# Square-root iteration of 1024 matrices with a convolution behind it: in images 19 to 31 the first quartic's square is turned by VectorE and DMA instead of TensorE

## The chip, the core and the metric

The kernel runs on one core of one Trainium2 chip, as one program. The metric is the time of one execution on the device in microseconds (us). A core has five engines with queues of their own: TensorE (PE; its weight loads are listed apart as PEld), VectorE (DVE), ScalarE (ACT), GpSimd (POOL) and SyncE (SP), and 16 DMA engines that move data between the chip's large memory (DRAM here) and its working memory SBUF, or inside SBUF. TensorE writes to PSUM, which has eight banks of 128 x 512 numbers.

## What is computed

x has 32 images of 32 channels of 128 x 128 numbers. Two layers are computed; only the first matters for this change. Cut down:

```python
def _L0_conv_ref(A):                      # A: 1024 matrices of 128 x 128
    normA = sqrt(sum(A2 * A2)); Y = A2 / normA; Z = I
    for _ in range(5):
        T = 0.5 * (3.0 * I - Z @ Y)
        Y = Y @ T
        Z = T @ Z
    return Y * sqrt(normA)

x = x + _L0_conv_ref(_gn(x))              # _gn: group norm, 16 groups of 2 channels
x = x + _L1_conv_ref(_gn(x), weights1, weights2)   # FFT, products by weights, inverse FFT
```

All numbers are 32-bit floats. Each matrix product of the first layer is four instructions of one bank: four channels form a group, and an image has eight groups.

## The kernel before, in words

The five iterations are rewritten as polynomials (`newton`, line 462). A group first gets a quartic polynomial q of its normalized matrix m, then y = m q, then the next m from y and q, then a second quartic of that, and at the end two short products that give the square root, which is added to the input tile xt. Since m isn't symmetric, a product needs one factor in transposed form; mb is the transposed companion of m.

There are two ways to make a quartic. `near_quartic` (line 407) is used for image 0 and images 19 to 31: v = square of m less a multiple of m, out of PSUM by DVE; r = mb + eye on POOL; v transposed by TensorE (`transposed(v)`: four instructions against the identity); w = that plus r, by DVE; then the product v w plus eye gives q. `far_quartic` (line 442) is used for images 1 to 18 in both quartics: the bare square is turned out of PSUM by one DVE instruction that transposes 32 x 32 blocks (`turned`, line 421), written to DRAM (`away`), and read back in another order (`back`) so that the blocks change places; v is made apart, by a DVE multiply-add onto a tile that POOL prepared as eye_v - mb, and POOL makes eye_q - m. No TensorE transposition is needed there, but two DMAs of 256 KB per quartic.

The order of the work is written out by hand. Each group is a Python generator, a lane, and each `yield` ends its share of a round. The main loop (line 1115) goes round the lanes; every engine runs its instructions in the order in which the loop issues them. A near lane is started every 5 rounds, a far lane every 3 (`NEAR`, `FAR`, line 42), and at most five near ones are under way. `yield from rest` is two rounds. Between lanes the loop steps the staging of later groups (`staged`, line 375, which scales xt into m and the second input tile into mb), the statistics of later images (`prep`, which loads xs on ACT's queue), the work behind a finished group (`settle`: a store to mid, folds on POOL; `forward`, `spectrum`), the products with weights, and `inverse` (line 953), which loads 512 KB tiles yt and results ob, adds and stores out. When a lane is started, `stage` also calls `fetch` (line 366) for a later group: two loads of 256 KB, which stand on SP's queue for far images and on ACT's for the others. `FIRST` is 19, the first image of the late stage.

Tiles come from `four` (line 312): `rooms` gives for each name how many buffers lie in the pool that stays (first number) and how many in a pool that exists until 158 groups have settled (second number); after that only the first number is left. A tile waits until the last reader of the buffer it takes is done.

Of the kernel before, what the change touches and what calls it, by code (L numbers as in the profile page):

```python
# [36 lines left out]
P = 128  # L37
# [56 lines left out]
def conv_preact_kernel(  # L94
# [84 lines left out]
    def bank():  # L179
        return ps8.tile([P, 4, P], F32, tag="ps", name="ps")  # L180
# [38 lines left out]
    def kept(issued):  # L219
        return issued  # L220
# [84 lines left out]
        yield  # L305


    rooms = dict(b=(4, 6), xt=(10, 5), x=(3, 2), r=(4, 0), v=(3, 2), w=(3, 2), q=(4, 2))
    rooms.update(my=(4, 3), mb=(2, 4), t=(3, 2), y4=(2, 2), turn=(0, 4))
    turns = dict.fromkeys(rooms, 0)  # L310

    def four(tag, more):
        n, m = rooms[tag]
        shape = [P, 4, 2, P] if tag == "my" else [P, 4, P]
        if more:
            turns[tag] += 1
            if turns[tag] % (n + m) >= n:
                return early.tile(shape, F32, tag=tag + "_early", name=tag, bufs=m)
        return sets.tile(shape, F32, tag=tag, name=tag, bufs=n)
# [20 lines left out]
    def minus(eye, m, t):  # L340

        nc.gpsimd.tensor_tensor(t, eye, m, ALU.subtract)
        return t
# [13 lines left out]
    def is_far(b):  # L357
        return 0 < b < FIRST

    def has_more(b, g):  # L360

        return b * (C // 4) + g < MORE
# [1 line left out]
    raw = {}  # L364

    def fetch(b, g):
        queue = nc.sync if is_far(b) else nc.scalar
        xt, t = four("xt", has_more(b, g)), four("b", has_more(b, g))
        kept(queue.dma_start(out=t, in_=x[b, :, 4 * g : 4 * g + 4, :]))
        kept(queue.dma_start(out=xt, in_=xt_in[b, :, 4 * g : 4 * g + 4, :]))  # L370
        raw[b, g] = xt, t
# [3 lines left out]
    def staged(b, g, nm, sc, off, sn):  # L375

        m = four("x", has_more(b, g))
        xt, mb = raw.pop((b, g))

        def on_scalar(t, x, offset, scale, c):  # L380
            c = slice(c, c + 1)
            kept(
                nc.scalar.activation(t, x, AF.Identity, bias=offset[:, c], scale=scale[:, c])
            )

        for j in range(4):
            c = 4 * g + j
            if j < 2 or not is_far(b):
                kept(
                    nc.gpsimd.tensor_scalar(  # L390
                        m[:, j, :],
                        xt[:, j, :],
                        nm[:, c // 2 : c // 2 + 1],
                        sc[:, c : c + 1],
                        ALU.add,
                        ALU.mult,
                    )
                )
            else:
                on_scalar(m[:, j, :], xt[:, j, :], off, sc, c)  # L400
            on_scalar(mb[:, j, :], mb[:, j, :], off, sc, c)
            yield
        v = minus(eye_v, mb, four("v", True)) if is_far(b) else None
        ready.append((xt, m, mb, v))
        yield

# [14 lines left out]
    def turned(ps, more):  # L421

        t = four("turn", more)
        nc.vector.transpose(blocks(t), ps.rearrange("p c (i b) -> p b c i", b=4))
        return t
# [13 lines left out]
    def by_rows(t):  # L439
        return blocks(t).rearrange("p a c j -> p c a j")  # L440

    def far_quartic(m, mb, v, f, later, more):

        ps = products(m, mb)
        held = away(turned(ps, more))
        if later:
            yield
        nc.vector.scalar_tensor_tensor(v, ps, 1 / (9 * MS), v, ALU.mult, ALU.add)
        if not later:
            yield  # L450
        minus(eye_q, m, m)
        yield
        w = back(held, "w", more)
        yield
        yield from rest
        q = plus(products(v, by_rows(w)), 9 / (39 * MS**2 * f**2), m, "q", more)
        yield from rest
        return q

    rest = (None, None)  # L460

    def newton(g, sn, xt, m, mb, v, far, more):


        qf, et, eye_t = (QS, EYE_Q, eye_q) if far else (QF, EYE, eye)
        if far:
            q = yield from far_quartic(m, mb, v, 1.0, False, more)
        else:
            q = yield from near_quartic(m, mb, more)
        my = four("my", more)  # L470
        y = my[:, :, 0, :]
        nc.scalar.mul(y, products(q, mb if far else m), 1 / (MS * qf))
        yield from rest
        m = my[:, :, 1, :]
        ps = products(y, q) if far else products(q, y)
        if far:
            held = away(turned(ps, more))
            yield
            nc.scalar.mul(m, ps, MS / qf)
            yield  # L480
            mb = back(held, "mb", more)
            yield from rest
            yield from rest
            v = four("r", more)
            form = "p c (a j) -> p c a j"
            minus(eye_p.rearrange(form, a=4), by_rows(mb), v.rearrange(form, a=4))
            q = yield from far_quartic(m, by_rows(mb), v, TURNED, True, more)
            w, y4 = four("t", more), four("y4", more)
            nc.scalar.mul(w, products(q, by_rows(mb)), 1 / (MS * qf * TURNED))
            ps = products(q, y)  # L490
            for j in range(4):
                c = 4 * g + j
                nc.scalar.mul(y4[:, j, :], ps[:, j, :], sn[:, c : c + 1])
        else:
            nc.scalar.mul(m, ps, MS / qf)
            yield from rest
            mb = taken(transposed(m), "mb", more)
            yield from rest
            q = yield from near_quartic(m, mb, more)
            both = [bank().rearrange("p (j k) x -> p j k x", k=2) for _ in range(2)]  # L500
            for j in range(4):
                nc.tensor.matmul(both[j // 2][:, j % 2], q[:, j], my[:, j], start=True, stop=True)
            w, y4 = four("t", more), four("y4", more)
            for h in range(2):
                nc.scalar.mul(w[:, 2 * h : 2 * h + 2, :], both[h][:, :, 1, :], 1 / (MS * qf))
            for j in range(4):
                c = 4 * g + j
                nc.scalar.mul(y4[:, j, :], both[j // 2][:, j % 2, 0, :], sn[:, c : c + 1])
        yield from rest
        t = plus(products(w, q), -0.5 * et / (1.5 * qf), eye_t, "t", more)  # L510
        yield from rest
        ps = products(y4, t) if far else products(t, y4)
        nc.vector.tensor_tensor(xt, ps, xt, ALU.add)
        if not todo and lanes.count(None) == LANES - 1:
            warm(2)
        yield
# [598 lines left out]
    while todo or any(lanes) or posts or specs or prods or backs:  # L1115
        tail = not todo and not any(lanes)
        if early and len(settled) >= MORE:
            change()
        for i in range(LANES):
            step(norms)  # L1120
            step(loads)
            far = todo and is_far(todo[0][0])
            under_way = [is_far(lane[0]) for lane in lanes if lane]
            room = far or under_way.count(False) + 0.6 * under_way.count(True) < LESS
            if lanes[i] is None and todo and room and rounds >= due:
                due = max(due, rounds - 1) + (FAR if far else NEAR)
                while norms:
                    step(norms)
                b, g = todo.pop(0)
                xt = ready[0][0]  # L1130
                lanes[i] = (b, g, xt, newton(g, made[b][3], *ready.pop(0), far, has_more(b, g)))
                if stages:
                    stage()
                if not todo:
                    loads.append(weights())
            if lanes[i] is not None:
                b, g, xt, steps = lanes[i]
                if (b, g) == (B - 1, C // 4 - 1):
                    steps_of_last.append(rounds)
                if next(steps, lanes) is lanes:  # L1140
                    lanes[i] = None
                    end(b, g, xt)
            if i == 1 and (early or rounds % 2):
                step(preps)
            if i == 2 or tail:
                step(specs)
            if i == 3 or tail:
                step(posts)
            turn = rounds % 10 in (0, 3, 7)
            if i == 0 and not turn or tail:  # L1150
                step(prods)
            if i == 0 and (turn or holding) or tail and not (posts or specs):
                step(backs)
        rounds += 1
# [69 lines left out]
```

## Time and profile before

| what | us or share |
|---|---|
| median of 3 runs (2980.7 to 2986.93) | 2981.98 |
| the profiled execution | 2981.79 |
| its span, first to last instruction | 2980.0 |
| granted TensorE clock, mean | 0.988 |
| PE busy | 2849.7 (96%) |
| PEld busy | 2663.8 (89%) |
| DVE busy | 2285.7 (77%) |
| POOL busy | 1988.4 (67%) |
| ACT busy | 1541.3 (52%) |
| DMA queue of SP (q1), share of 16 engines' time | 59.9% |
| DMA queue of ACT (q10) | 13.7% |
| the chain of work that ended last: PE | 72% |
| DMA, DVE in the same chain | 12%, 9% |

Busy time is the time in which an engine works at least at one instruction; a product that waits for its operands counts as idle. Because TensorE's instructions are pipelined, the distance between starts tells more than the length of one. An instruction group is printed as out<-in by the names of the tiles: "ps<-ident,v" are the transposes of v, "ps<-w,v" the products of v and w, "ps<-x,b" the squares of the first quartic of a near group, and "w<-turn" the DMA that brings a turned tile back. The number after x is how many there were. Behind the bar stand busy time and mean length of one in ns; then the idle time of the engine ahead of them with what ended it. Nearly all instructions carry the line of a helper (L88), so the groups are told apart by their tiles.

By time, the span falls into the far stage (to about 1530 us; the last turned tile is at 1529.6), and the late stage: the first quartics of groups 152 to 255 begin at 1494 us and end at 2873. The inverse transforms of the first 20 images run beside the late stage from about 1830 us, when the first yt is loaded.

### The profile page before, as it was taken

The numbers are of one execution on the slowest core, as the hardware profiler recorded it, in microseconds if no ns is written. First come the engines' busy times: TensorE is split into PE (matmuls) and PEld (weight loads), VectorE is DVE, ScalarE is ACT, GpSimd is POOL, SyncE is SP. The second block draws the span as 40 slices with busy tenths as digits, with TensorE's granted clock in tenths as the row PEclk, the third lists the DMA queues.
The fourth block names the chain that finished last, engine by engine and source line by source line (L and its number), as shares of the span: only waits on it lengthen the run. The fifth ranks groups of instructions, "written<-read, shape, count | busy, mean of one in ns | idle before, by whom it ended". The sixth has DMA issues, their size and how long they took to land.

```text
span 2980.0 us, 73661 instructions
## 1 busy us (share of the span) xinstructions
PE 2849.7 (96%) x27688; PEld 2663.8 (89%) x27688; DVE 2285.7 (77%) x4407; ACT 1541.3 (52%) x3899; POOL 1988.4 (67%) x2308
## 2 busy tenths in 40 slices
PE   7999999999999999999999999999999999999995
PEld 7899999999999899999999888888888899888983
DVE  7878898889788888888876545886876876777665
ACT  4555555555555555555544445545555544655452
POOL 4667767777777767767755534777777763678452
PEclk9999999999999999999999999999999999999997
DMA  5688889888888889898943566867877737666567
GB/s 177 199 280 272 253 267 281 275 266 282 269 275 257 283 253 294 253 291 255 303 139 104 157 203 208 284 231 242 281 242 248 261 124 226 209 230 218 186 211 268
DMA packets 566897, 711.90 MB, mean 239 GB/s; under 512 B 94736, under 2 KB 329232, under 8 KB 566544
## 3 DMA queue, kind: packets, MB, share of 16 engines
q1 hardware_dynamic: 494400, 574.26, 59.9%
q10 hardware_dynamic: 72144, 132.94, 13.7%
q8 instruction: 221, 3.62, 0.5%
q14 instruction: 132, 1.08, 0.1%
HBM read 440.17 MB, written 266.86 MB: 237 GB/s over the span
## 4 chain that ended last, share of the span: by engine, by line
PE 72%; DMA 12%; DVE 9%; issue 2%; POOL 2%; ACT 1%; SPq 1%; ACTq 0%; DVEq 0%; POOLq 0%
PE ps L88 72%; DMA xs<-in_xs 3%; DMA w<-turn 3%; DVE yt L88 1%; DVE turn L88 1%; DMA turn<-turn 1%; DVE b_d L88 1%; DMA yt<-mid 1%; DMA ob<-od 1%; DVE a_st L88 1%; DVE root L88 1%; DVE q L88 1%; DVE b_st L88 1%; SPq L88 1%; DVE v L88 1%
## 5 line engine op out<-in xcount | busy, mean ns | idle before, releaser
L88 POOL TENSOR_TENSOR fold<-xt 128x256 f32<-128x256 f32 x512 | 364.1, 734 | 308.4 <-DVE xt L88 274.2
L88 ACT ACTIVATE b<-b,a_off,a_sc 128x128 f32<-128x128 f32 x1024 | 467.2, 492 | 127.2 <-issue 27.9
L88 ACT ACTIVATE my<-ps 128x512 f32<-128x512 f32 x512 | 302.4, 602 | 410.4 <-PE ps L88 278.0
L88 PE MATMUL ps<-my,q 128*128 128x128 f32 (+1 forms) x2944 | 475.9, 309 | 6.5 <-ACT my L88 6.4
L88 POOL TENSOR_TENSOR yt<-yt,d 128x512 f32<-128x512 f32 x244 | 306.6, 1283 | 212.3 <-ACT d L88 192.8
L88 PEld LDWEIGHTS ps<-my,q 128*128 128x128 f32 x2944 | 411.9, 191 | 35.4 <-ACT my L88 7.6
L88 PE MATMUL ps<-w,v 128*128 128x128 f32 x2944 | 399.2, 279 | 26.1 <-DMA w<-turn 11.9
L88 POOL TENSOR_TENSOR v<-eye_v,b 128x512 f32<-128x512 f32 x144 | 184.0, 1278 | 352.2 <-ACT b L88 316.2
L88 ACT ACTIVATE t<-ps 128x256 f32<-128x256 f32 (+1 forms) x368 | 171.1, 467 | 462.8 <-PE ps L88 447.2
L88 PEld LDWEIGHTS ps<-w,v 128*128 128x128 f32 x2944 | 362.2, 193 | 41.7 <-issue 10.5
L88 POOL TENSOR_SCALAR x<-xt,a_nm,a_sc 128x128 f32<-128x128 f32 x736 | 323.7, 456 | 15.3 <-DVE a_sc L88 15.0
L88 DVE STREAM_TRANSPOSE turn<-ps 128x512 f32<-128x512 f32 x432 | 295.4, 698 | 45.3 <-PE ps L88 36.9
L88 ACT ACTIVATE y<-ps,a_t_s 128x128 f32<-128x128 f32 x1024 | 292.2, 372 | 42.9 <-PE ps L88 42.7
L88 PE MATMUL ps<-q,t 128*128 128x128 f32 x2048 | 273.4, 277 | 1.3 <-DVE r L88 1.3
L88 PEld LDWEIGHTS ps<-q,t 128*128 128x128 f32 x2048 | 249.0, 192 | 4.2 <-DVE r L88 1.5
L88 DVE BATCH_NORM_STATS2 a_st<-xs 128x6 f32<-128x256 f32 x504 | 184.9, 409 | 77.9 <-DMA xs<-in_xs 77.5
L88 DVE SCALAR_TENSOR_TENSOR w<-ps,r 128x512 f32<-128x512 f32 x224 | 152.9, 683 | 108.7 <-PE ps L88 75.3
L88 DVE SCALAR_TENSOR_TENSOR q<-ps,eye 128x512 f32<-128x512 f32 x224 | 153.3, 684 | 94.2 <-PE ps L88 90.1
L88 DVE TENSOR_TENSOR xt<-ps,xt 128x512 f32<-128x512 f32 x256 | 174.4, 681 | 50.6 <-PE ps L88 48.2
L88 POOL TENSOR_TENSOR r<-mb,eye 128x512 f32<-128x512 f32 x112 | 143.1, 1278 | 86.3 <-ACT mb L88 86.3
L88 DVE TENSOR_TENSOR yt<-ps,yt 128x512 f32<-128x512 f32 x256 | 163.0, 681 | 46.5 <-PE ps L88 40.9
L88 DVE BATCH_NORM_STATS2 b_st<-xt 128x6 f32<-128x256 f32 x512 | 188.0, 407 | 0.5
(147 smaller groups left out, 6296.5 us busy)
## 6 DMA issues: line engine op xcount, KB each, us to landing
turn<-turn SPq DMA_DIRECT2D x432, 256.0 KB
w<-turn SPq DMA_DIRECT2D x288, 256.0 KB
mid<-xt SPq DMA_DIRECT2D x256, 256.0 KB
yt<-mid SPq DMA_DIRECT2D x128, 512.0 KB
xs<-in_xs ACTq DMA_DIRECT2D x252, 256.0 KB
out<-yt SPq DMA_DIRECT2D x115, 512.0 KB
b<-in_x SPq DMA_DIRECT2D x144, 256.0 KB
xt<-in_xt SPq DMA_DIRECT2D x144, 256.0 KB
```

What stands on the lines that cost most here:

```text
L88: return self.tc.keep_in_program_order(issue(*args, **kw))
```

## The change

Groups of images 19 to 31 make their first quartic in a new way, `late_quartic`; the second quartic stays `near_quartic`. The square (with the factors of the product exchanged) is turned out of PSUM by DVE, and `across` moves it from one SBUF tile to another with four DMAs on SP's queue, each of which reads 32 partitions and writes 128, 512 bytes a piece. v is prepared in `staged` by POOL as eye_v - m, and the square is added to it by DVE. POOL makes eye_q - mb in place. There is no transposition of this quartic on TensorE, and r is not made. As a consequence two of the four channels of m are scaled on ACT instead of POOL (as in far groups), the loads of `fetch` stand on SP's queue for all images but the first, and `newton` uses far constants for the first half of these groups and near ones for the second. Some buffers move between the two pools: q from 4 and 2 to 3 and 3, t from 3 and 2 to 2 and 3, turn from 0 and 4 to 2 and 2.

```diff
-    rooms = dict(b=(4, 6), xt=(10, 5), x=(3, 2), r=(4, 0), v=(3, 2), w=(3, 2), q=(4, 2))
-    rooms.update(my=(4, 3), mb=(2, 4), t=(3, 2), y4=(2, 2), turn=(0, 4))
+    rooms = dict(b=(4, 6), xt=(10, 5), x=(3, 2), r=(4, 0), v=(3, 2), w=(3, 2), q=(3, 3))
+    rooms.update(my=(4, 3), mb=(2, 4), t=(2, 3), y4=(2, 2), turn=(2, 2))
...
+    def is_late(b):
+        return b >= FIRST
...
     def fetch(b, g):
-        queue = nc.sync if is_far(b) else nc.scalar
+        queue = nc.sync if b else nc.scalar
...
-            if j < 2 or not is_far(b):
+            if j < 2 or not b:
...
-        v = minus(eye_v, mb, four("v", True)) if is_far(b) else None
+        v = minus(eye_v, mb if is_far(b) else m, four("v", has_more(b, g))) if b else None
...
+    def across(t, more):
+
+        w = four("w", more)
+        for a in range(4):
+            src = t[32 * a : 32 * a + 32].rearrange("p c x -> p (c x)")
+            kept(
+                nc.sync.dma_start(
+                    out=w.rearrange("p c x -> p (c x)")[:, P * a : P * a + P],
+                    in_=src.rearrange("p (b x) -> p b x", b=4),
+                )
+            )
+        return w
+
+    def late_quartic(m, mb, v, more):
+
+        ps = products(mb, m)
+        w = across(turned(ps, more), more)
+        nc.vector.scalar_tensor_tensor(v, ps, 1 / (9 * MS), v, ALU.mult, ALU.add)
+        yield
+        minus(eye_q, mb, mb)
+        yield
+        yield from rest
+        q = plus(products(v, by_rows(w)), 9 / (39 * MS**2), mb, "q", more)
+        yield from rest
+        return q
...
-    def newton(g, sn, xt, m, mb, v, far, more):
+    def newton(g, sn, xt, m, mb, v, far, late, more):
...
-        qf, et, eye_t = (QS, EYE_Q, eye_q) if far else (QF, EYE, eye)
+        qf, et, eye_t = (QS, EYE_Q, eye_q) if far or late else (QF, EYE, eye)
         if far:
             q = yield from far_quartic(m, mb, v, 1.0, False, more)
+        elif late:
+            q = yield from late_quartic(m, mb, v, more)
         else:
             q = yield from near_quartic(m, mb, more)
...
             q = yield from near_quartic(m, mb, more)
+            qf, et, eye_t = QF, EYE, eye
```

## The prediction

> **What bounds the kernel now.** First I read the busy time of each engine by stretches: a far stretch (images 1 to 18), the densest late stretch, the whole late stage, and the end.
>
> ```profile
> 200.00:1400.00 1200.00, 1172.17 (x10611) 1132.57 (x10611) 1020.15 (x2002) 647.16 (x1662) 881.32 (x976) 1.00 0.86 272
> 1900.00:2400.00 500.00, 480.27 (x4233) 433.98 (x4234) 389.55 (x714) 262.16 (x691) 389.19 (x448) 0.99 0.73 250
> 1550.00:2900.00 1350.00, 1305.67 (x13797) 1191.40 (x13796) 947.82 (x1763) 698.82 (x1748) 861.00 (x1041) 0.99 0.65 213
> 2900.00:2980.00 80.00, 46.00 (x508) 30.22 (x506) 42.36 (x74) 23.61 (x55) 27.57 (x24) 0.76 0.77 271
> ```
>
> The columns after the length are PE, weight load, DVE, ACT and POOL busy, then the granted clock, DMA share and GB/s. In the late stage, which is what changes, TensorE works 1306 of 1350 us. DVE has 70%, ACT 52%, POOL 64%. So TensorE bounds it, with 44 us of gaps.
>
> Next the weight loads of this stage, which show what a transpose costs there against a product:
>
> ```profile
> L88 PEld LDWEIGHTS ps<-x,b 128*128 128x128 f32 x800 | 97.4, 192 | 1.6 <-DVE w L88 0.8 <-issue 0.5
> L88 PEld LDWEIGHTS ps<-ident,v 128*128 128x128 f32 x812 | 95.4, 143 | 16.8 <-issue 10.0 <-DVE v L88 3.4 <-DVE b_st L88 0.4
> L88 PEld LDWEIGHTS ps<-ident,my 128*128 128x128 f32 x408 | 47.0, 141 | 1.9 <-DVE w L88 0.8 <-issue 0.7
> ```
>
> A product of four matrices is eight instructions (two for each), a transposition of four is four instructions. The busy time over the count is 0.115 to 0.12 us an instruction.
>
> Then one group (four channels) of an image whose inverse transforms run beside it, in order of time, from its square to the next use of its v:
>
> ```profile
> 2079.74 0.97 PEld L88 LDWEIGHTS ps<-x,b 128*128 128x128 f32 x8
> ...
> 2080.83 0.33 ACTq L88 DMA_DIRECT2D b<-in_x  x1
> 2081.20 0.45 ACTq L88 DMA_DIRECT2D xt<-in_xt  x1
> ...
> 2081.83 1.65 SPq L88 DMA_DIRECT2D yt<-mid  x2
> ...
> 2083.09 0.68 DVE L88 SCALAR_TENSOR_TENSOR v<-x,ps 128x512 f32<-128x512 f32 x1
> 2083.58 1.50 SPq L88 DMA_DIRECT2D ob<-od  x2
> ...
> 2083.89 0.42 PEld L88 LDWEIGHTS ps<-ident,v 128*128 128x128 f32 x4
> 2084.43 0.97 PEld L88 LDWEIGHTS ps<-y,t 128*128 128x128 f32 x8
> ...
> 2090.01 1.08 PEld L88 LDWEIGHTS ps<-w,v 128*128 128x128 f32 x8
> ```
>
> The four transposes stand at 2083.89 and the next product follows at 2084.43: 0.42 us of loads, 0.54 us of the sequence. The product v*w of this group comes at 2090.01. In the changed kernel w has to get out of PSUM, through DVE, through SP's queue and back into SBUF in that time, behind two 512 KB loads of yt.
>
> **What goes.** Groups 152 to 255 are 104 groups; each loses one transposition of four: 416 instructions. At 0.105 (0.42/4 in the timeline) it is 43.7 us, at 0.1175 (95.4/812) 48.9 us. I take 0.11: **46 us** less on TensorE, the engine that sets the end of this stage. The second quartic keeps its two transpositions.
>
> **DVE.** It loses v (0.686) and w (0.682), keeps q, and gains the turn out of PSUM (0.70, the far rows turn<-ps) and the multiply-add onto v (0.65, the far rows v<-ps,v): 0.02 us less a group. Nothing.
>
> **POOL.** It loses r (1.28) and two of four scalings (2 x 0.455), and gains eye_v - m and eye_q - mb (2 x 1.28): 0.37 us a group, 38 us in all. It lies beside TensorE: 861 + 38 of 1350 us, and 78% becomes 81% in the dense stretch. Its result is also wanted later: r was wanted one round after its issue (DVE waits for r 19.7 us in this stage), eye_q - mb is wanted three rounds after. Price nothing; if the cover were gone, at most 38 us.
>
> **ACT.** It gains two scalings (2 x 0.49) and loses the issue of two loads (0.335 and 0.445, medians of the late rows): 0.2 us a group, 21 us beside 699 of 1350. Nothing; uncovered, 21.
>
> **SP.** It gains the two loads and four tile-to-tile transfers, six issues of 0.33 to 0.45: about 2.2 us a group, 230 us on top of 347 us of issuing in 1350. It is no bound by busy time. What counts is order: SP waits in line, and the late stage already shows for what.
>
> ```profile
> SPq L88 <- DVE xt L88: 295.3, 45, 13.3
> SPq L88 <- POOL yt L88: 147.5, 56, 4.7
> SPq L88 <- PE ps L88: 104.0, 61, 6.0
> SPq L88 <- DMA yt<-mid: 93.4, 42, 6.0
> ```
>
> The last line is a landing that SP waits for before it may issue something else. In the program all DMAs of both queues use eight completion semaphores in turn, and an issue waits for the landing of the eighth before it. The stage issues 0.75 DMAs per us, afterwards about 1.06, what the far stretch has (1.03). Queued behind a waiting transfer are stores of mid and out, yt loads, and the next w; ACT's xs loads share the eight, and my copies stand behind these.
>
> **The new wait: is w there in time?** I followed each of the 104 groups through the trace, by four readings: the end of the first quartic's v on DVE (the turn will end about there), the end of the last SP issue ahead of it in program order, the latest landing of those, and the start of v*w on TensorE. From v's end to the need there are 8.4 us at the median, 6.4 in the tightest tenth. The reckoning: the loads now in front add 0.85 of issuing; the last of four issues comes 1.15 later; a 64 KB transfer lands 2.3 after that (diag<-in_wk, also 64 KB, lands 2.7 after issue at the median, 1.7 at the least). Or, if something is ahead in the rings, w lands after that landing plus its own packets: 512 of 512 B at 27 ns (the trace's packet records of that size, nearly all w<-turn and mb<-turn) over 16 engines, 0.9 us, plus 1.35 for the two loads (256 packets of 2 KB at 84 ns over 16) if these count again.
>
> By the first rule alone 2 groups of 104 are late, 1.3 us in sum. By the second, with the loads, 13 are late, 21.7 us; nearly all follow an out and two yt, like the one above, which comes out 3.2 us late. Since 0.11 x 4 x 0.8 groups leave the way in between, the need comes 0.35 us earlier: 26.5 with the loads, 12.4 without. One more us for all groups gives 44 and 25. Tile-to-tile transfers have no row here; the bounds are 1 us quicker (11) and 2 us slower (68). I take **20 us**, between the two ways of counting the loads, and bounds 4 to 68. For: two such trips per quartic cost the far stretch only this, at a DMA share of 0.86:
>
> ```profile
> PE ps L88 <- DMA w<-turn: 15.7, 16, 3.2
> ```
>
> Against: there the need is five rounds off, not four, and no 512 KB loads come in bursts.
>
> Two rules of the Trainium skill bear on this. "SBUF — State Buffer", section "Door 1: The DMA port swizzle", states that partitions 0 to 31 reach 8 of 16 ports, about 218 GB/s; each of the four transfers reads 32 partitions. As an estimate from that page 64 KB would take 0.30 us where the packets' row gives 0.22, so w would land 0.35 us later and 26.5 would become 32. No run shown settles it. "DMA: Bandwidth & Descriptors", section "Rules for kernel authors", says that spreading DMAs over issuing engines gains no bandwidth, only issue time; by it the loads were ahead of w before too, the 1.35 is counted twice, and 12.4 is the figure.
>
> **Rooms.** In the late stage q has 3 buffers (two live four rounds in five), t 2, turn 2 (each free well before the next use), v 3 of which 13 of 15 buffer-rounds are taken; the freeing reader is a round ahead in each case. Price nothing, bound 5 us. At the end a wk load into the third q may wait two rounds: 0 to 3 us.
>
> **Sum.** The profiled execution has 2981.8 us, its span 2980.0, its median of runs 2982.0, so no shift. 2981.8 - 46 + 20 + 1 = **2957**.
>
> **Rivals.** (a) w is in time throughout, as in the far stretch: -46 + 4 (the first rule with one us more), **2940**. For: by that rule only 2 groups are late; DMA share only 0.65. Against: the 13 groups. (b) Slower: the bursts decide. If issues wait for the eighth landing before them, then at 1.4 times the issue rate w, xs and yt delay each other; w lands 4 us later, 143 us of lateness of which feedback (a stalled TensorE stretches the next need) leaves perhaps half, 72: 2981.8 - 46 + 72 = **3008**. It decides from 1.35 us on top of the reckoning (44 us eats the gain). For: the two landing waits above. Against: the far stretch lives with the same issue rate. (c) The change does what it says, but TensorE's gaps refill: DVE to TensorE steps two rounds apart have 3% less time, and 44 us of gaps grow; gain halved and w at 20: **2979**, the same.
>
> **How the numbers follow.** Forecast 0.47, (a) 0.18, (b) 0.24, (c) 0.11. A difference under 0.2% (6 us) can't be told from no change here. Faster: forecast and (a), 0.65; same 0.11; slower 0.24. The range runs from (a) with 49 us gone and 4 us of waits, 2936, to 60 us of waits, 2996, about the upper bound of w's price (68) with a little feedback, and so into (b); beyond it lies about 0.15, below it 0.05.
>
> **What the profile would show.** ps<-ident,v falls from x896 to x480; TensorE waits for DMA w<-turn some 13 to 20 times, 1 to 3 us each, in groups behind yt; SP's waits for yt landings grow; POOL at 81 to 83% in the dense stretch with no TensorE wait on it. Wrong if w's waits are over 46 us in sum, if ACT waits for landings before my, or if DVE waits for POOL's v.

## The result, and the profile after

The changed kernel takes 2990.9 us (median of 20 runs, 2984.6 to 3013.1), the kernel before in the same session 2983.0 (20 runs, 2975.5 to 2994.7). The ratio is 1.0028, 95% interval [1.0015, 1.0041]: slower, by some 8 us. The prediction was faster by 25. The two profiled executions took 2981.8 and 2997.0 us, so the readings of the profiles below have 15 us of difference to explain, not 8.

First the two late stretches of the changed kernel, with the columns of the prediction's first view (length, then PE, weight load, DVE, ACT and POOL busy, granted clock, DMA share, GB/s):

```profile
1900.00:2400.00 500.00, 463.86 (x4017) 417.90 (x4016) 375.59 (x700) 280.43 (x748) 396.72 (x402) 0.97 0.79 263
1550.00:2900.00 1350.00, 1266.12 (x13255) 1150.69 (x13253) 925.62 (x1748) 756.16 (x1920) 889.01 (x932) 0.97 0.72 229
```

TensorE has less to do, but isn't done earlier: in 1350 us it works 1266 instead of 1306, and its idle time goes from 44 to 84 us. The granted clock falls from 0.99 to 0.97, a column that the prediction did not price. The weight loads of the same stage show that the work did go:

```profile
L88 PEld LDWEIGHTS ps<-ident,v 128*128 128x128 f32 x404 | 47.6, 143 | 12.2 <-issue 6.2 <-DVE v L88 1.7 <-DVE xt L88 1.6
```

812 had become 404 (896 and 480 in the whole run). What TensorE waits for in the late stage of the changed kernel (us in total, times, longest):

```profile
PE ps L88 <- DMA w<-turn: 20.5, 13, 4.2
PE ps L88 <- DVE t L88: 9.8, 11, 1.8
PE ps L88 <- DMA plain<-xs: 9.8, 5, 4.2
PE ps L88 <- DMA diag<-xs: 8.8, 2, 5.6
```

In the same answer of the kernel before, w<-turn and DVE t are not there, and of plain and diag it has:

```profile
PE ps L88 <- DMA diag<-in_wk: 7.4, 4, 2.9
...
PE ps L88 <- DMA plain<-xs: 3.3, 2, 1.9
...
PE ps L88 <- DMA diag<-xs: 1.1, 1, 1.1
```

The first line of the changed kernel is the wait that the prediction priced at 20. The other three belong to work that the change doesn't touch: t of the lane's second half, and the operands of the products with weights, which SP loads.

One late group, in order of time (start, length, engine, operation, tiles, how many; in brackets idle time before it):

```profile
2348.21 1.22 SPq L88 DMA_DIRECT2D yt<-mid  x2
...
2349.01 0.70 DVE L88 STREAM_TRANSPOSE turn<-ps 128x512 f32<-128x512 f32 x1
2349.64 0.65 DVE L88 SCALAR_TENSOR_TENSOR v<-ps,v 128x512 f32<-128x512 f32 x1
2350.22 0.67 DVE L88 SCALAR_TENSOR_TENSOR t<-ps,eye 128x512 f32<-128x512 f32 x1
2350.61 4.44 SPq L88 DMA_DIRECT2D w<-turn  x4
2351.04 1.13 PE L88 MATMUL ps<-y,t 128*128 128x128 f32 x8 [1.10 <-DVE t L88]
...
2359.58 2.05 PE L88 MATMUL ps<-w,v 128*128 128x128 f32 x8 [2.60 <-DMA w<-turn]
2361.42 0.85 PE L88 MATMUL ps<-ident,v 128*128 128x128 f32 x3
```

Three losses stand in it. The turn and the multiply-add onto v stand together on DVE ahead of t, and y*t waits 1.10 us for t. The four issues of w hold SP for 4.44 us, behind two yt loads, and v*w waits 2.60. And v*w then takes 2.05 us for what takes 1.06 elsewhere in the same stage. The stretches around that wait, from the same trace, say why (PE busy, granted clock, DMA share, GB/s):

```profile
2352.79:2356.97 4.18, 4.18 (x35) 1.00 0.92 318
2356.97:2359.50 2.53, 0.00 (x1) 1.00 0.89 268
2359.50:2362.90 3.40, 3.32 (x15) 0.50 0.88 281
2362.90:2365.50 2.60, 2.60 (x27) 1.00 0.75 229
```

After 2.5 us in which TensorE does nothing, the granted clock is 0.50 for 3.4 us: in that time 1.7 us of work are lost, and nothing is waiting any more.

So the late stage is taken apart into three. Each row of the table is worked out from one profile: from the first to the last square of a first quartic, the time in which neither products nor weight loads run (gaps, and how many of them are over 1.5 us), the windows of 3.4 us with halved clock and the time lost in them (half of the time in which TensorE ran there), and the rest, which is TensorE's work at full clock. The last column adds up TensorE's waits for plain and diag, the operands of the products with weights, in the window 1550 to 2900. The runs are those of the experiments below.

| run | stage | gaps (over 1.5 us) | halved windows, us lost | rest | plain, diag |
|---|---|---|---|---|---|
| before | 1370.2 | 42.1 (10) | 6, 9.8 | 1318.3 | 11.8 |
| changed | 1386.0 | 81.1 (20) | 20, 30.0 | 1274.9 | 24.0 |
| a4_no_transposes | 1344.1 | 50.7 (12) | 12, 18.2 | 1275.2 | 10.5 |
| a1_no_move | 1336.0 | 47.5 (11) | 11, 16.4 | 1272.1 | 11.2 |
| c1_one_copy_unread | 1338.2 | 50.8 (12) | 9, 14.2 | 1273.2 | 9.2 |
| f2_two_copies_unread | 1338.5 | 50.0 (10) | 10, 15.6 | 1272.9 | 13.8 |
| d1_four_copies_unread | 1357.7 | 65.0 (16) | 13, 19.6 | 1273.2 | 21.0 |
| f1_four_slivers_unread | 1356.2 | 63.7 (16) | 13, 19.7 | 1272.7 | 23.8 |
| a2_move_unread | 1354.6 | 65.6 (17) | 10, 14.5 | 1274.5 | 27.9 |
| g1_every_second_group | 1379.9 | 65.6 (13) | 10, 15.4 | 1298.9 | 18.2 |

The rest falls by 43.4 us in the changed kernel and by 44 to 46 in the unread and unmoved ones. In the changed kernel the gaps grow by 39.0 and the time lost to halved clock by 20.2: together 59.2, more than the gain.

### The profile page after: what moved, and what is told of

Read it like the earlier page. It is cut to its first block, busy times and chain, and to the rows that moved or that the text cites. A ratio compares the mean times of both kernels' runs of the same rounds, so it can differ in the third digit from the quotient of the medians.

```text
span 2995.2 us, 73837 instructions
## 1 busy us (share of the span) xinstructions
PE 2823.8 (94%) x27272; PEld 2634.8 (88%) x27272; DVE 2270.1 (76%) x4407; ACT 1609.3 (54%) x4107; POOL 2026.2 (68%) x2204
## 5 line engine op out<-in xcount | busy, mean ns | idle before, releaser
L88 ACT ACTIVATE b<-b,a_off,a_sc 128x128 f32<-128x128 f32 x1024 | 484.0, 494 | 64.3 <-DMA turn<-turn 20.2
L88 DVE STREAM_TRANSPOSE turn<-ps 128x512 f32<-128x512 f32 x536 | 369.8, 701 | 98.0 <-PE ps L88 91.8
L88 POOL TENSOR_TENSOR v<-eye_v,x 128x512 f32<-128x512 f32 x104 | 132.6, 1275 | 384.0 <-ACT x L88 218.1
L88 ACT ACTIVATE x<-xt,a_off,a_sc 128x128 f32<-128x128 f32 x496 | 244.6, 493 | 5.6 <-DMA xt<-in_xt 2.1
L88 POOL TENSOR_SCALAR x<-xt,a_nm,a_sc 128x128 f32<-128x128 f32 x528 | 233.0, 452 | 15.2 <-DVE a_sc L88 15.0
L88 POOL TENSOR_TENSOR r<-eye_p,mb 128x512 f32<-128x512 f32 x144 | 183.8, 1276 | 2.9 <-DMA mb<-turn 2.9
```

The source lines that it names most:

```text
L88: return self.tc.keep_in_program_order(issue(*args, **kw))
```

## The experiments

Each kernel was timed in five rounds against the kernel before on the same chip; ratios are to that, with 95% intervals. 1% is 30 us.

### What the parts cost

My theory after the result was that the transposes give what was reckoned, and that the move takes it back in two ways: by w's lateness, and by standing in SP's queue ahead of other transfers. The rival was that the transposes had been worth little.

**a1_no_move**: the product reads the turned tile itself. The move is left out, so the 32 x 32 blocks stand in wrong places in q.

```diff
-        w = across(turned(ps, more), more)
+        w = turned(ps, more)
```

> The changed kernel without the tile-to-tile transfers: v*w reads the turned tile itself, so the four DMAs and the wait for them are gone and the product gets blocks in the wrong places. Theory W (TensorE waits for w to land, and each stall of about 2 us is followed by a stretch at half clock): 46 us under the kernel before plus a few, about 2940, with few half-clock stretches in the late stage. Theory Q (the loads that moved to SP's queue) or P (POOL's and ACT's staging work) alone: stays over 2975. Theory Z (the transposes were never worth 46 us, the gaps refill): about 2983.

Measured: 2953.8 us, 0.9897 [0.9873, 0.992]. Without the move the change is worth 31 us, between what the theories gave, and 11 halved windows stay.

**a2_move_unread**: as a1, but the four transfers are made, into a tile that nobody reads.

```diff
-        w = across(turned(ps, more), more)
+        w = turned(ps, more)
+        across(w, more)
```

> The changed kernel with the four transfers still issued into w, but v*w reads the turned tile: all traffic and all queue positions stay, only the wait of TensorE for the landing goes (the product gets blocks in the wrong places). Theory W: as without the transfers, 2940 to 2950. If the transfers hurt by delaying yt, xs and stores behind them: 2965 to 2985.

Measured: 2978.2, 0.997 [0.9953, 0.9988]. The transfers cost 22 us (0.0073) although nobody waits for them; that the product waits for w costs the other 17 (1.0028 - 0.997). By the intervals these two prices are known to some 9 and 7 us. In a2 TensorE waits 27.9 us for plain and diag, in a1 11.2.

**a4_no_transposes**: the kernel before, with the first quartic's transposition of v left out in images 19 to 31; w is made from the square as it stands in PSUM, so its data are not the reference's.

```diff
-        w = plus(transposed(v), 1.0, r, "w", more)
+        w = plus(ps if bare else transposed(v), 1.0, r, "w", more)
```

> The kernel before without the four transposes of the first quartic in images 19 to 31: w is made from the square itself in PSUM instead of the transposed v; nothing else moves. Theory W: TensorE's 46 us come off nearly whole, 2935 to 2945. Theory Z: 2965 or more.

Measured: 2963.5, 0.9925 [0.9898, 0.9952]: 22 us (14 to 30), where the rest column falls by 43.1. So the rival has about a half of the truth. The work of the transposes is there as reckoned, but in the profile 9 us come back as gaps and 8 as halved clock, with no move in the kernel at all. One thing besides the transposes differs: the bank of the square is held until w is made, two rounds longer. What that costs isn't known.

**a3_loads_on_act**: the changed kernel with the loads of images 19 to 31 on ACT's queue, as before.

```diff
-        queue = nc.sync if b else nc.scalar
+        queue = nc.sync if is_far(b) else nc.scalar
```

> The changed kernel with the loads of images 19 to 31 back on ACT's queue. Theory Q (the loads ahead of w on SP and their wait for the buffer b, which q now frees): 2950 to 2965. Theory W in general: w comes about 0.85 us earlier, some 10 of the 18 late groups stay late: 2975 to 2985.

Measured: 3007.0, 1.0079 [1.006, 1.0098]. Slower than the changed kernel by 0.5%, which neither theory expected: moving the loads to SP was not what cost. w is hardly earlier (waits for w<-turn 18.1 us, 13 times), and TensorE now waits 9.4 us for ACT's my.

### Can w be made to come in time?

**b1_move_first**: the lane's first step, and with it the move, is issued ahead of the loads of `stage` in late images.

```diff
+                held = stages and is_late(b)
-                if stages:
+                if stages and not held:
                     stage()
...
+                if held:
+                    stage()
```

> The changed kernel with the staging call, and so the two loads of a later group, put behind the lane's first step for images 19 to 31: the four transfers of w now stand ahead of the loads on SP's queue, and of the loads' wait for buffer b. Theory W (w's landing is what is late): w lands some 1 to 3 us earlier, about 8 of the 18 late groups stay late, 2976 to 2984 where the changed kernel has 2995 and the kernel before 2986. If the order on SP's queue does not matter: 2990 to 2996.

Measured: 3002.1, 1.0051 [1.0033, 1.0069], slower than either expectation. w's waits fall to 11.9 us (7 times), and waits for plain<-xs and diag<-xs rise to 25.1: what is put behind the four issues is late in w's place.

**b2_later_need**: b1, with v*w one round later and `LESS` (how many near lanes may be under way) raised from 5 to 6, since lanes are longer.

```diff
         minus(eye_q, mb, mb)
         yield
+        yield
         yield from rest
```

> As with the transfers ahead of the loads, and v*w of the first quartic one round (about 2.6 us) later, so that a lane lasts 26 rounds and six near lanes may be under way. Theory W: hardly a group is late; the time falls to that of the transfers that nobody waits for, 2972 to 2980. If the longer lanes cost more in buffers and banks than the waits did: 2985 or more.

Measured: 2996.6, 1.0026 [1.0007, 1.0046], as the changed kernel. w's waits are 10.3 us, but diag<-in_wk has 16.9 and plain<-in_wk 11.0.

**b3_need_from_rest**: b1 with v*w one round later, the round being taken from the two behind q.

```diff
+        yield
         yield from rest
         q = plus(products(v, by_rows(w)), 9 / (39 * MS**2), mb, "q", more)
-        yield from rest
+        yield
```

> As with the transfers ahead of the loads, and v*w one round later, but the round is taken from the two between q and its use, so that a lane stays 25 rounds long. Theory W with room to spare behind q: 2972 to 2980. If q needs its two rounds: TensorE waits for DVE's q instead, 2985 to 2995.

Measured: 3023.2, 1.0125 [1.01, 1.0151], 28 us over the slower expectation. The wait has moved to the next step of the lane:

```profile
PE ps L88 <- DVE q L88: 34.9, 19, 5.1
```

**f3_later_need_loads_first**: the edit of b3 without b1, run later.

> The whole changed computation with the loads ahead of the move as in the changed kernel, the product v*w one round later, and the wait behind q cut from two rounds to one so that the length of the work stays. My theory (w's lateness costs some 0.6%, the move's issues the rest): w's gaps of 24 us fall to under 8, and the quick q costs new ones of 10 to 15 as it did with the loads moved behind: 2980 to 2998. If lateness of w alone had made the change slow: 2960 to 2972.

Measured: 3017.8, 1.0108 [1.0086, 1.013]. My number (2980 to 2998) was missed: w's waits still are 10.9 us and q's are 34.7, over twice what I gave them.

**d2_by_dram** and **d3_by_dram_loads_first**: the move by way of DRAM, with two transfers of 256 KB instead of four of 64 KB, as in the far stage. d2 is made from b2, the way back issued two rounds after the way out; d3 has the loads first again.

```diff
-        w = across(turned(ps, more), more)
+        held = away(turned(ps, more))
...
+        w = back(held, "w", more)
         yield
```

> A whole version: the first quartic of images 19 to 31 turns its square by way of DRAM as the far images do, two DMAs with about 0.7 us of issuing in place of 2.4; w is wanted one round later, six near lanes, and the loads stand behind the lane's first step. If SP's time held up the loads of weights and spectra that TensorE waits for: most of that goes, w is in time, 0.4 to 1% under the kernel before, 2957 to 2975. If the two trips are too long for five rounds: w late as before or worse, 2990 or more.

> The same, but the loads stay ahead of the lane's first step, as in the changed kernel. Theory W: w comes up to 2 us later than with the loads behind, 5 to 10 us slower. If the order on SP decides nothing, or the loads are what is short: equal or faster.

Measured: 3112.1, 1.0415 [1.0398, 1.0432], and 3133.6, 1.0484 [1.047, 1.0498]. Two landings in a row are far too slow for this place; from d2:

```profile
PE ps L88 <- DMA w<-turn: 98.5, 41, 5.7
```

That also prices lateness: the gaps over 1.5 us number 41 in d2 and 44 in d3, the halved windows 38 and 42.

### Why four unread transfers cost

**c1_one_copy_unread** and **d1_four_copies_unread**: the product reads the turned tile (blocks in wrong places), and the same 256 KB are copied plainly to a tile nobody reads, by one transfer or by four (the edit of d1 is shown).

```diff
-        w = across(turned(ps, more), more)
+        w = turned(ps, more)
+        copied = four("w", more)
+        for j in range(4):
+            kept(nc.sync.dma_start(out=copied[:, j, :], in_=w[:, j, :]))
```

> The changed kernel, v*w reading the turned tile (blocks in the wrong places), and in place of the four transfers one plain copy of the turned tile into w, of the same 256 KB, which nobody reads. Without any transfer it was 1.0% under the kernel before, with the four unread ones 0.3%. If the number of issues costs these 0.7% (SP's issuing time, or the eight landing semaphores): 0.8 to 1.0% under the kernel before, 2956 to 2962. If the bytes in the rings cost it: 0.3 to 0.4% under, 2974 to 2978.

> The changed kernel, v*w reading the turned tile (blocks in the wrong places), with four plain copies of a quarter of the turned tile each into w, which nobody reads: as many issues, landing semaphores and bytes as the change has, but in the plain form, whose issue should take SP about 0.33 us in place of 0.6. One plain copy gave 1.2% under the kernel before, the four real transfers unread 0.3%. If the number of DMAs (eight semaphores in turn) makes the difference: about 0.3% under, 2977 to 2981. If SP's time for these issues makes it: more than half of the way back, 0.8 to 1.2% under, 2953 to 2965.

Measured: one 2951.4, 0.9878 [0.9852, 0.9904], as without any move; four 2981.6, 0.9973 [0.9958, 0.9987], as a2. So neither the bytes cost, nor, in a transfer that nobody reads, the pattern of 32 partitions read and 128 written. I had expected plain issues to be shorter than those of the move; they aren't.

**f1_four_slivers_unread** and **f2_two_copies_unread**: as d1, with 512 bytes from one partition in each of the four, or with two half copies.

```diff
-            kept(nc.sync.dma_start(out=copied[:, j, :], in_=w[:, j, :]))
+            kept(nc.sync.dma_start(out=copied[0:1, j, :], in_=w[0:1, j, :]))
...
-        for j in range(4):
-            kept(nc.sync.dma_start(out=copied[:, j, :], in_=w[:, j, :]))
+        for j in range(2):
+            kept(nc.sync.dma_start(out=copied[:, 2 * j : 2 * j + 2, :], in_=w[:, 2 * j : 2 * j + 2, :]))
```

> The turned tile is read directly by the product (blocks in wrong places), and four transfers per group of one partition's 512 bytes each, read by nobody, stand on SyncE's queue where the four quarter copies stood. As many transfers, issues and completion slots as with the quarter copies (0.9973 of the kernel before), almost no bytes and one row each. If the cost of four is the count alone (their slots, or a fixed time of issuing each): 2976 to 2984, as the quarter copies. If it is the time that SyncE takes to write out 128 rows four times, and that time falls with the rows: issues under 0.4 us and 2953 to 2965, some 1% below before. The issue's length in the trace belongs to the answer: unchanged at 0.6 us it leaves issuing time and count unseparated.

> As with the quarter copies, but two plain half copies of 128 KB per group, read by nobody (blocks in wrong places). One copy gave 0.9878 of the kernel before, four gave 0.9973. If each further transfer costs alike: 0.991 to 0.993, 2960 to 2967. If two are still hidden in SyncE's spare time as one is: 0.987 to 0.989, 2949 to 2955. If the second transfer starts the whole cost: 0.995 to 0.998.

Measured: four slivers 2971.0, 0.9946 [0.9925, 0.9967], between the two expectations; two halves 2953.4, 0.9884 [0.9863, 0.9905]. Two cost nothing, four cost, nearly whatever they carry (f1 and d1 are 0.0027 apart, about the uncertainty of that difference, and their late stages take 1356 and 1358 us). The issues on SP's queue, of c1, d1 and f1 in turn (ns min/median/max):

```profile
L88 SPq DMA_DIRECT2D w<-turn x100: 470/492/1903, 1561.8 to 2836.5; - x100
```

```profile
L88 SPq DMA_DIRECT2D w<-turn x404: 464/594/1612, 1553.0 to 2864.6; - x135
```

```profile
L88 SPq DMA_DIRECT2D w<-turn x400: 497/581/1927, 1557.2 to 2852.2; - x134
```

A transfer from tile to tile takes SP 0.49 to 0.59 us to issue, with 128 rows or with one. The place of the loss is the last column of the table: with none, one or two transfers TensorE waits 9 to 14 us for plain and diag, with four 21 to 28. That is 10 to 17 of the 16 to 18 us by which the gaps grow from a1 to d1, f1 and a2: a good part of what SP issues behind four comes too late for the products.

**e1_plain_on_act**: the copies of d1 on ACT's queue, one round later, to tell SP's issuing time (theory S) from the number of transfers under way, each waiting for a completion slot (theory L).

```diff
         yield
+        copied = four("w", more)
+        for j in range(4):
+            kept(nc.scalar.dma_start(out=copied[:, j, :], in_=w[:, j, :]))
```

> The turned tile is read directly by the product, and four plain quarter copies into w, read by nobody, are issued on ScalarE's queue one round later (blocks in wrong places in the product). Against the same copies on SyncE (0.9973 of the kernel before) and one copy on SyncE (0.9878): theory S gives 2953 to 2965, about 1% below before, since SyncE's issuing is as without them; theory L gives 2977 to 2981, 0.2 to 0.4% below before, since as many transfers are under way. ScalarE's 2.4 us of issuing per group lie in its spare time by both.

**d4_across_split**: the whole changed computation, two of the four transfers on ACT's queue.

```diff
-                nc.sync.dma_start(
+                (nc.scalar if a % 2 else nc.sync).dma_start(
```

> The changed kernel with two of the four tile-to-tile transfers of a group issued on ScalarE's queue and two on SyncE's, same place, same reader. Theory S (SyncE's issuing time is what four transfers cost): SyncE issues some 1.2 us less per group, the last of the four stands 1.2 us earlier, so the late w's fall from 18 to some 6 and the products' loads come in time more often: 0.3 to 0.6% below the changed kernel, that is 2972 to 2982. Theory L (the number of transfers that are under way, each waiting for a completion slot, is what they cost): nothing is relieved there, ScalarE only gets some 1.2 us more per group to issue, 2988 to 3000.

**e2_across_act_late**: all four on ACT's queue a round later, v*w a round later, `LESS` 6.

```diff
-                nc.sync.dma_start(
+                nc.scalar.dma_start(
...
-        w = across(turned(ps, more), more)
+        t = turned(ps, more)
...
         yield
+        w = across(t, more)
         minus(eye_q, mb, mb)
         yield
+        yield
```

> The whole changed computation with the four tile-to-tile transfers on ScalarE's queue, issued one round after the turn, and the product v*w a round later, with one step fewer of lead elsewhere. Theory S: SyncE as in the kernel without a move, w in time nearly always: 2955 to 2970, faster than both kernels. Theory L: 2978 to 2996.

Measured: e1 3034.7, 1.0153 [1.0129, 1.0177]; d4 3097.6, 1.0362 [1.0341, 1.0382]; e2 3052.2, 1.0216 [1.0195, 1.0236]. Both theories missed all three, and a sentence they shared was wrong: that ACT's time for issuing was spare. ACT works in line too, and TensorE's operands stand in that line. From d4, ACT around its two issues:

```profile
1947.02 0.71 DVE L88 STREAM_TRANSPOSE turn<-ps 128x512 f32<-128x512 f32 x1
...
1947.76 1.21 ACTq L88 DMA_DIRECT2D w<-turn  x2
...
1949.02 0.88 ACT L88 ACTIVATE b<-b,a_off,a_sc 128x128 f32<-128x128 f32 x2 [5.66 <-DVE t L88]
```

DVE's turn of this group ends at 1947.73 (1947.02 + 0.71), and the issue starts at 1947.76: ACT has stood for it, 5.66 us in all with the issue. In e1, where the turn is long done, it is the issue itself, and at times an earlier landing, that holds ACT back:

```profile
1963.47 2.48 ACTq L88 DMA_DIRECT2D w<-turn  x4
1965.99 0.65 ACT L88 COPY d<-ps 128x256 f32<-128x256 f32 x2 [2.00 <-DMA w<-turn]
```

By the profile, SP waited in e1's window 1550 to 2900 for an earlier landing 206 times, 333 us in sum, against 170 times and 138 us in d1, though the copies were no longer on its queue. The two queues take completion semaphores in one common turn, so one queue can wait for what the other has under way; that this is the reason isn't shown by a run.

So whether four issues on SP cost by their time or by the landings that later issues wait for isn't settled by an experiment: f1 kept both. One comparison speaks for the time: in f2 SP waits for landings as long as in d1 (174 times, 163 us), and two copies cost nothing, while SP's issues take 582 us of the same window in f2 and 703 in d1.

**g1_every_second_group**: the whole computation, with the change in every second group of images 19 to 31 only.

```diff
-    def is_late(b):
-        return b >= FIRST
+    def is_late(b, g):
+        return b >= FIRST and g % 2 == 1
```

Loads, v and the scaling of the other groups are as in the kernel before.

> The whole computation with the change made in every second group of images 19 to 31 alone (52 of 104 groups, loads of these on SyncE), and the other groups as in the kernel before. Half of the transposes go (23 us), and SyncE has four transfers per two groups, two per group on average, which cost nothing where they were half copies read by nobody. My theory, a threshold in SyncE's issuing and half as many late w's: 0.991 to 0.997 of the kernel before, 2960 to 2980, faster than both kernels. If the cost is proportional to the number of transfers, with the gain halved too: 1.000 to 1.002, 2986 to 2996.

Measured: 2992.7, 1.0025 [1.0011, 1.0039]. My theory of a threshold in the mean rate of issues falls; the other expectation, a cost in proportion, is met. Against before, the rest is 19.4 us less (half of 43.4 would be 21.7) and gaps and halved clock together 29.1 more (half of 59.2 is 29.6); w is waited for 11 times, 12.8 us. So the loss goes with the number of moved groups, and spreading them thinner helps nothing.

No whole version beat the kernel before; those that did leave the transposes out, or the blocks in wrong places.

## Why the prediction was wrong

**What goes: right.** 416 transposes at 0.11 us were to be 46; the rest column fell by 43.4 in the changed kernel, 43.1 in a4 and 44 to 46 where nothing is read from the move. The error is not here.

**The step that failed first: work taken from TensorE was taken off the time one for one.** a4 took the transposes away, and of 43 us of work 22 reached the time. The steps of a lane are a fixed number of rounds apart; with shorter rounds, operands have less time to arrive. That reading isn't tested by itself. What a4's profile shows for it is that products wait longer for DVE's q (10.7 us against 6.8) and t (11.5 us, one wait of 7.8 among them, against none). This is the mechanism of rival (c), which I gave 0.11. It was about half, as (c) put it, and (c) had no halved clock in it.

**The clock: not in the sum at all.** The granted clock stood in the prediction's own first view, 0.99 in the late stage against 1.00 in the far one, and no question was asked of it. All 14 stretches of halved clock in the late stage of the changed kernel, each of one or two windows of 3.4 us, begin during a gap of 1.7 us or more or within 3 us behind it. The rows of the table have 0.6 to 1 halved window for each gap over 1.5 us. So a wait of 2 to 3 us that brings such a window costs up to 1.7 us more than its own length. In the changed kernel against before this is 20.2 us.

**The new wait for w: right in size, partly by luck.** 13 late groups and 20 us were forecast; the wait is seen 13 times, 20.5 us. a2 against the changed kernel says 17 us of time. Ten of the 13 late groups stand behind two yt, as foretold; the two longest waits (4.2 and 3.7 us) don't, there SP had issued diag<-xs and od<-om ahead of the move. And the way itself was longer than reckoned: the issue of one tile-to-tile transfer took 0.60 us, not 0.33 to 0.45, so the last of four started 1.93 us after the first at the median, not 1.15, and one of these transfers landed 3.4 us after its issue (median of 400), where the prediction's 64 KB row has 2.7. By the prediction's own count one more us for all groups would have given 25 to 44 us; why it came to 20 all the same is not shown.

**SP: wrong.** "It is no bound by busy time. What counts is order" was followed for w alone. The order also puts the operands of the products, plain and diag, behind the four issues. That is a2 against a1: 22 us, in a sum that had 0 for it. This term decides the side: the 31 us of a1 less the 17 of w's wait would still have been some 14 us faster. Nor did SP's waits for yt landings grow; in the late stage they went from 93.4 to 38.8 us, for which no run gives the reason.

**DVE: wrong by place.** The sum of its durations is unchanged as reckoned, but two instructions now stand where one stood, ahead of t, and the products wait 9.8 us for t in 11 groups; in a1 it is 19.2. How much of it the place makes is not shown, since a4, whose DVE works as before, has 11.5.

**POOL and ACT: right as far as seen.** POOL has 79% in the dense stretch (I said 81 to 83), and TensorE's products wait 2.9 us for ACT's my (6.4 before). Two waits of the weight loads, 7.7 us, that the profile puts down to POOL's x are new; I have not followed them.

**The rivals.** (b) has the side but not the mechanism at its size: w's waits are 20 us, not 72. The result is (a sum worked out from the ratios) -31 for the change without the move, of which the transposes alone are 22, +22 for four transfers in SP's queue, +17 for waiting for w: +8. Each term is known to 7 to 9 us. Of the signs that I named as "wrong if", w's waits over 46 us and DVE waiting for POOL's v did not appear, and ACT's waits for landings before my are there (13.8 us) but are less than in the kernel before (31.0). They guarded the terms that were not at fault.

The Trainium skill's rule that I weighed, eight ports for 32 partitions ("SBUF — State Buffer", section "Door 1: The DMA port swizzle"), decided nothing: four plain copies over 128 partitions (0.9973) cost what four reads of 32 partitions cost (0.997). A rule that I did not weigh speaks to the point: "DMA: Bandwidth & Descriptors", section "Rules for kernel authors", advises one transfer over 128 partitions in place of two over halves, because they share the same engines anyway. The pieces here are cut by columns, not by partitions, so the runs don't try that very case. Here one copy cost nothing and four of the same bytes 0.95%, though two cost nothing either.

## What to carry to other kernels

When an engine that sets the end is relieved, first run the kernel with that work simply left out: it shows how much of the gain the order of the work lets through (here some 22 of 46 us) before the price of the new way is paid. Price a transfer by what stands behind it on its issuing engine, not only by when its own data come: four small ones in a row cost about as much in others' lateness (22 us) as in their own (17). And a wait on TensorE is to be priced with the clock that it can cost afterwards.

## What the runs showed of the hardware

Halved clock after short waits. In all 20 profiles, the kernel before among them, stretches of granted clock 0.50 in the late stage come in units of 3.4 us, somewhat fewer than the gaps over 1.5 us: 6 for 10 in the kernel before, 20 for 20 in the changed one, 13 for 16 in d1, 22 for 25 in e1, 25 for 29 in e2, 30 for 33 in d4, 38 for 41 in d2, 42 for 44 in d3. The traces also tell which gaps count. Within one profile these stretches begin whole multiples of 3.41 us apart, so I laid such a grid over the late stages of the 20 profiles and added up TensorE's idle time (neither products nor weight loads) in each window. After a window at full clock with 2.0 us or more of idle time the next one was halved in 214 of 214 cases, with 1.7 to 2.0 us in 40 of 87, with less in 4 of 7501; after a halved window 0.6 us kept it halved in 101 of 101, less in 3 of 259. So a gap that is shared by two windows can go free: two of the four gaps of 2.5 to 2.9 us in the kernel before have no halved window behind them. "TensorE: Matmul & The Clock Gate", section "Why this matters for your kernels", advises "No PE-idle gaps >~3µs between matmul bursts"; here 2 us of idle time in one window were enough, so the bound to reckon with is lower. That the idle time causes the windows is read from their order and their numbers; no run set a gap by itself.

Issues from tile to tile are slow. SP takes 0.49 us for a single copy and 0.58 to 0.60 for one of several in a row, against 0.34 and 0.43 for its loads of b and xt from DRAM in the changed kernel (medians, 1550 to 2900), and 512 bytes take as long as 64 KB (f1 and d1). Where a transfer's source is not ready, the issuing engine stands, and everything behind it: ACT in d4 was idle for 5.66 us.
